# A graph-attention kernel on one core: two loads put behind the twelfth store of G, batch 1's row flags computed in the loop and sent through memory

## The chip, the cores and the metric

The kernel runs on one core of one Trainium2 chip, in float32. The metric is device time in microseconds (us) of one execution; the core's engines are TensorE (PE: matmuls, with PEld for its weight loads), VectorE (DVE), ScalarE (ACT), GpSimd (POOL) and SyncE (SP), which issues most of the DMAs.

## The reference

Sixteen batches of 512 rows with 512 features each. `v` is x, `q` one vector per batch, `adj` an integer tensor with 11 labels per pair; NONGT is 20, H is 16.

```python
row_zero = v.sum(-1) == 0
q_exp = where(row_zero[..., None], 0.0, q[:, None, :])
self_feat = concatenate([v, q_exp], -1) @ W_self.T + b_self
output = self_feat
for d in range(2):
    A = (adj_f if d == 0 else swapaxes(adj_f, 1, 2))[:, :, :NONGT, :]
    cond, vb = A.sum(-1), A @ w_bias + b_bias
    # attention of 512 queries over the first 20 rows, 16 heads of 32
    aff = einsum('bnhd,bmhd->bnhm', qh, kh) / sqrt(32)
    aff = where(cond > 0, aff, -9e15) + vb
    w = softmax(aff, -1)
    output += per-head projection of (w @ self_feat[:, :20]) by Wout[d] + bout[d]
return v + relu(output)
```

The row flags of this document are the negation of `row_zero`: the query vector enters a row of `self_feat` only where the row of x has a sum other than zero.

## The kernel before, in words

Features lie on the partitions, in four chunks of 128 (`C`); a batch's 512 rows are the columns, worked in four tiles of 128 (`nt` 0 to 3).

**Setup** (lines 458 to 777). The weights are loaded, the features of the 20 key rows of all batches are computed, and Wq is folded into the keys: `keys(runs)` (667) makes G, the keys of all batches as seen from the features, in 20 bursts `n` = 0 to 19 of TensorE products into two pairs of PSUM banks. ACT and DVE evict a burst into staging tiles `st` (four buffers), and SP stores each finished stage to memory, two stores to each of the 16 stages (698, 699). Between the bursts a list `plan` (721) sets other work for TensorE, by letters: m, b, c biases; v, w the projected values (`values`, 640); n the row flags (`row_flags`, 211); p the seven products of batch 0's `self_feat`. Lines 752 to 777 hang work of other engines on single bursts: masks (`mask_mul`, `mask_count`, `mask_sum`, `mask_spread`), `row_sums(1)`, `x_sum`, `clear_first` and `spill`.

**Row flags.** For batches 0 and 1, `row_sums` adds the four chunks of x on POOL; `row_flags` multiplies a 128x128 tile of ones with the sum, which leaves each row's total on all 128 partitions, and DVE compares with zero straight into `nz`. From batch 2 on ACT sums rows of x in another layout, POOL compares (`row_mask`, 195), SP stores the 512 flags to memory (198) and loads them back to all partitions (`load_nz`, 200).

**self_feat by seven products.** `product(b, n)` (250) computes a batch's features by a Strassen-like scheme of seven half-size products with sums of x blocks (`x_sum`, POOL). Products 1, 6, 7 and 4 accumulate in two banks `ps_a`; after each of them DVE reads the banks as they stand, with the flags: `partial` (285) adds `nz * qw` and writes a block of `sf`. Each further product onto `ps_a` waits for the partial before it. Product 2 goes to `ps_d`, 5 and 3 to `ps_c`; `joined` adds them.

**The main loop** (797). For each tile: the scores of 128 rows against G in two halves (`scores`, 349; 32-output products, four abreast), then `weigh` on DVE (add to the mask tile `full`, maximum, subtract), `expo` on ACT, and one tile later `normal` (sum and reciprocal on DVE, multiply on POOL) and `turn` (DVE transpose). At `nt` = 2 the previous batch is finished: `attend` (426) multiplies transposed weights with the projected values `vd`, in six runs of four products per batch, 32 or 64 outputs wide, and `finish` adds, applies relu and stores. The products of batch b+1 are woven in: 1 and 2 at `nt` = 2, with the first partial run by DVE between the maximum and the subtraction of that tile (939); 6, 7 and 5 at `nt` = 3; 4 and 3 at `nt` = 0 of the next batch.

**The order of everything is written by hand** (`manual_schedule`): each engine's instructions and SP's DMAs go out in program order. `behind` adds a wait that ties a load to an instruction of the loop. A DMA on SP also waits for the landing of the DMA eight places before it.

**Values' way.** The projected values `vw_d` are copied into a block pattern `bd_d` in memory, over zeros (`clear_first`, `clear_rest`), by small DMAs: `spill` (184) issues the next ones of a list. For the first five batches there are twelve: six from POOL in bursts 14 to 19 (765), six from POOL at `nt` = 0 of batch 0 (862).

**Memory pools.** After setup the pools `soft`, `gp`, `work`, `xsum` and `ident` (780 to 784) lie, in that order, over memory that setup used; a first write waits for the last use of what was there.

Of the kernel before, what the change touches and what calls it, by code (L numbers as in the profile page):

```python
# [7 lines left out]
F32 = mybir.dt.float32  # L8
I32 = mybir.dt.int32
AF = mybir.ActivationFunctionType  # L10
ALU = mybir.AluOpType
AX = mybir.AxisListType

P = 128
# [4 lines left out]
def gat_kernel(  # L19
# [20 lines left out]
    nc = tc.nc  # L40
    B, F, N = xT.shape
# [166 lines left out]
        for k in range(2, C):  # L208
            nc.gpsimd.tensor_add(t, t, xs[b][:, k])

    def row_flags(b):
        ps = bank(f"ps_nz{b}")
        nc.tensor.matmul(ps[:, :N], ones, rss[b], start=True, stop=True)  # L213
        nzs[b] = load.tile([P, N], F32, tag="nz", name=f"nz{b}")
        nc.vector.tensor_scalar(nzs[b], ps[:, :N], 0.0, None, ALU.not_equal)


    def weight_sums():
# [207 lines left out]
    def attend(b, banks, tiles=slice(0, NT), start=True, stop=True):  # L426


        wt = wts[b][:, tiles].rearrange("p t (g w) -> p (t g) w", g=HL)
        vd = vds[b].rearrange("p e i g -> p (e i g)")  # L430
        for first, runs in ((True, ((0, 1, 0), (3, 1, 2), (4, 1, 2), (7, 1, 4))), (False, ((1, 2, 1), (5, 2, 3)))):
            for at, n, j in runs:
                for a in range(HL):
                    r = bass.ts(a, R)
                    nc.tensor.matmul(  # L435
                        banks[a][bass.ds(at // 2 * DH, n * DH)].rearrange("p (t n) -> p t n", n=32),
                        vd[r, bass.ds(at * DH, n * DH)], wt[r, :, bass.ts(j, 32)],
                        start=start and first, stop=stop and not first,
                    )
# [18 lines left out]
    with tc.tile_pool(name="setup", bufs=1) as sp, tc.tile_pool(name="ps_acc", bufs=4, space=PSUM) as acc["pool"]:  # L458
# [18 lines left out]
        with tc.tile_pool(name="setup_k", bufs=1) as sk:  # L477
# [46 lines left out]
            nc.sync.dma_start(bo_sb, bout)  # L524
            for d in range(2):
                rows(wo_sb[:, d], woT[d])
            load_x(1)
            load_adj(0, 1)


            nc.gpsimd.tensor_add(rsk, xkv[:, 0], xkv[:, 1])
# [86 lines left out]
        with tc.tile_pool(name="setup_g", bufs=4) as sg:  # L618
# [82 lines left out]
            def block_product(n):  # L701
# [11 lines left out]
                "b": [(biases, ())],  # L713
                "c": [(bias_scores, (d,)) for d in range(2)],
                "m": [(bias_terms, (d, c)) for c in range(C) for d in range(2)],
                "n": [(row_flags, (b,)) for b in range(2)],
                "p": [(block_product, (n,)) for n in (1, 2, 6, 7, 5, 4, 3)],
                "v": [(values, (t, (d,), k)) for t in range(2) for d in range(2) for k in range(C)],
                "w": [(values, (2, (0, 1), k)) for k in range(C)],
            }  # L720
            plan = "mmvv bvv vvc vvc vvn vvw vvw vw wn p p p p p p p".split()

            units = [(fc, hg, d, b) for fc in range(C) for hg in range(C) for d in range(2) for b in range(B)]
            bursts = []
# [11 lines left out]
            for n, runs in enumerate(bursts):  # L736
                for i in range(len(rest)):
                    if i < (4 if n == 0 else 1) or any(fc == 0 and (d, hg) == rest[0] for fc, hg, d, _, _ in runs):
                        key_rows(*rest.pop(0))
                if n == 4:  # L740
                    values(*steps["v"].pop(0)[1])
                keys(runs)
                if rest:
                    for kind in "mm" if n else ():
                        f, args = steps[kind].pop(0)
                        f(*args)
                    continue
                first = n if first is None else first
                for kind in plan[n - first] if n - first < len(plan) else ():
                    f, args = steps[kind].pop(0)  # L750
                    f(*args)
                if n == 7:
                    mask_mul(0, 0)
                if n == 8:
                    mask_count(0, 0)
                if n == 10:
                    mask_sum(0, 0)
                    load_cq(0)
                if n == 7:
                    clear_first()  # L760
                if n == 9:
                    row_sums(1)
                    copies = blocks(0)
                if n > 13:
                    spill(1, nc.gpsimd)
                if n == 11:
                    new_self(0)
                    for i in range(1, 5):
                        x_sum(0, i)
                if 10 < n < 15:  # L770
                    mask_spread(0, 0, (n - 11,))
                if n == 14:
                    mask_mul(0, 1)
                if n == 15:
                    mask_count(0, 1)
                if n == 17:
                    full_add(0, 0)

    acc["pool"] = ctx.enter_context(tc.tile_pool(name="ps_loop", bufs=1, space=PSUM))
    soft = ctx.enter_context(tc.tile_pool(name="soft", bufs=2))  # L780
    gp = ctx.enter_context(tc.tile_pool(name="gp", bufs=2))
    work = ctx.enter_context(tc.tile_pool(name="work", bufs=2))
    xsum = ctx.enter_context(tc.tile_pool(name="xsum", bufs=1))
    ident = ctx.enter_context(tc.tile_pool(name="one", bufs=1)).tile([P, P], F32, name="ident")

    with tc.manual_schedule():
# [10 lines left out]
        for b in range(B):  # L797
# [7 lines left out]
            for nt in range(NT):  # L805
# [13 lines left out]
                if nt == 0:  # L819
# [39 lines left out]
                        turn(*prev)  # L859
                    full_add(b, 1)  # L860
                    if b == 0:
                        spill(6, nc.gpsimd)
                    if more:
                        x_sum(b + 1, 1)
                        load_adj(b + 1, 0, done["xsum"], slice(1, 2))
# [41 lines left out]
                if nt == 2:  # L907
# [22 lines left out]
                        load_xn(b + 2, 1, done["sum"], slice(1, 2))  # L930
                    if more:
                        load_keys(b + 1, range(1), done["normal"])
                    for g in range(2):
                        scores(b, nt, g, ps[g])
                    if more:
                        product(b + 1, 1)
                        product(b + 1, 2)
                        new_self(b + 1)
# [147 lines left out]
```

## Time and profile before

| what | value |
|---|---|
| device time, median of 3 runs | 583.28 us (582.72 to 583.82) |
| the profiled execution | 582.57 us |
| its span, first to last instruction | 580.7 us |
| mean granted TensorE clock | 0.999 |
| DMA, mean over the span | 212 GB/s, 123.26 MB |

A row of the chain of waits has the start in us from the span's start, the length, and the engine, tile and line. A row of a timeline has start, length, engine, line, operation and tiles, with the idle time ahead of it and what ended it in brackets. A row of the stretches has the stretch, its length, the busy time of each engine with the count of its instructions, the granted clock, and share and rate of the DMA.

### The profile page before, as it was taken

Reading aid. Unit: us, or ns where it says so; the run is one execution under the profiler, and the core shown is the slowest. Engines: PE = TensorE matmul, PEld = TensorE weight load, DVE = VectorE, ACT = ScalarE, POOL = GpSimd, SP = SyncE. Lnnn points to the kernel's source line nnn. Section 1 sums busy time; section 2 is a strip of 40 time slices with the busy share of each in tenths; the row PEclk is TensorE's granted clock in tenths of the full one; section 3 lists DMA queues with packets and bytes.
Section 4 is the critical chain, followed back from the end, with each engine's and each line's share of the span. In section 5 each row is a group of like instructions: output and inputs, shape, how many; then the busy total and the mean of one; then the engine's idle time right before and its main releaser. Section 6 shows DMA issues by size and latency. Waiting matters only on the chain.

```text
span 580.7 us, 30994 instructions
## 1 busy us (share of the span) xinstructions
PE 574.0 (99%) x13496; PEld 431.6 (74%) x13496; DVE 489.8 (84%) x786; ACT 395.8 (68%) x1170; POOL 404.2 (70%) x383
## 2 busy tenths in 40 slices
PE   8999999999999999999999999999999999999996
PEld 6444458878878787878778787887887878787873
DVE  0475676979898989898999999898989898989896
ACT  1334454587877777778786868687887877777671
POOL 2626976748687776858585867786868677685875
PEclk9999999999999999999999999999999999999999
DMA  8998997857675767777576767566657666674404
GB/s 290 387 399 300 332 362 274 231 144 222 202 239 177 215 200 198 218 181 229 171 215 166 219 166 219 166 205 181 202 162 223 197 191 182 196 205 109 148 19 146
DMA packets 98787, 123.26 MB, mean 212 GB/s; under 512 B 18876, under 2 KB 66968, under 8 KB 96604
## 3 DMA queue, kind: packets, MB, share of 16 engines
q1 hardware_dynamic: 96124, 117.80, 65.5%
q0 software_dynamic: 1392, 2.43, 1.8%
q8 instruction: 106, 1.74, 1.2%
q10 hardware_dynamic: 1136, 1.06, 0.5%
q14 instruction: 29, 0.24, 0.1%
HBM read 82.30 MB, written 40.24 MB: 211 GB/s over the span
## 4 chain that ended last, share of the span: by engine, by line
PE 94%; DVE 3%; DMA 1%; issue 0%; POOL 0%; SPq 0%; ACT 0%; DVEq 0%; POOLq 0%; ACTq 0%
PE ps_s L365 45%; PE ps_a L283 19%; PE ps_c L283 9%; PE ps_o L435 5%; PE ps_d L283 5%; PE ps_v L649 3%; PE ps_k L588 3%; DMA ws_q<-in_wsT 1%; PE ps_kv L537 1%; DVE o L444 0%; PE ps_nz L213 0%; DVE o L1023 0%; DVE wt L424 0%; DVE ps_s L383 0%; DVE sm L415 0%
## 5 line engine op out<-in xcount | busy, mean ns | idle before, releaser
L365 PEld LDWEIGHTS ps_s<-g,sf 128*32 128x32 f32 x8192 | 263.0, 110 | 21.5 <-issue 13.9
L365 PE MATMUL ps_s<-g,sf 128*32 128x152 f32 x8192 | 278.1, 293 | 0.3 <-issue 0.2
L337 ACT COPY both<-add 32x80 f32<-32x80 f32 x512 | 130.9, 256 | 60.3 <-DVE add L328 54.4
L417 POOL TENSOR_TENSOR s<-s,sm 128x640 f32<-128x640 f32 x63 | 80.2, 1274 | 95.5 <-DVE sm L416 73.4
L344 POOL TENSOR_TENSOR full<-cq,both 128x640 f32<-128x640 f32 x64 | 100.3, 1567 | 27.1 <-issue 21.2
L317 ACT ACTIVATE prod<-adj,wb_sb 128x80 f32<-128x80 int32 x330 | 112.4, 432 | 0.0
L392 ACT ACTIVATE s<-s 128x640 f32<-128x640 f32 x63 | 46.5, 738 | 56.5 <-DVE s L387 56.1
L449 POOL TENSOR_TENSOR o<-o,x 128x512 f32<-128x512 f32 x60 | 76.6, 1299 | 0.0
L379 DVE TENSOR_TENSOR full<-ps_s,full 128x608 f32<-128x608 f32 x63 | 48.7, 773 | 22.5 <-PE ps_s L365 19.2
L283 PE MATMUL ps_a<-t,ws_s 128*32 128x246 f32 x1024 | 60.0, 371 | 0.0
L415 DVE TENSOR_REDUCE sm<-s 128x32 f32<-128x640 f32 x63 | 50.8, 807 | 10.6 <-ACT s L392 10.4
L383 DVE TENSOR_REDUCE ps_s<-full 128x32 f32<-128x640 f32 x63 | 52.2, 828 | 2.2
L424 DVE STREAM_TRANSPOSE wt<-s 128x640 f32<-128x640 f32 x63 | 52.8, 838 | 0.6 <-POOL s L417 0.6
L387 DVE TENSOR_TENSOR s<-full,ps_s 128x640 f32<-128x640 f32 x63 | 51.5, 818 | 1.1
L289 DVE SCALAR_TENSOR_TENSOR sf<-nz,qw,ps_a 128x246 f32<-128x246 f32 x128 | 51.6, 443 | 0.3
L283 PEld LDWEIGHTS ps_a<-t,ws_s 128*32 128x32 f32 x1024 | 33.9, 110 | 17.5 <-issue 0.9
L328 DVE TENSOR_REDUCE add<-prod 128x80 f32<-128x960 f32 x32 | 36.8, 1149 | 6.8 <-ACT prod L317 4.0
L446 ACT ACTIVATE o<-o,bo 128x512 f32<-128x512 f32 x60 | 38.2, 709 | 0.6 <-DVE o L444 0.6
L248 POOL TENSOR_TENSOR t<-x 128x492 f32<-128x492 f32 x32 | 36.7, 1148 | 1.6 <-DMA g_d<-st 1.5
L248 POOL TENSOR_TENSOR t<-x,t 128x492 f32<-128x492 f32 x32 | 36.7, 1148 | 1.3
L435 PE MATMUL ps_o<-wt,vd 32*32 32x512 f32 (+5 forms) x816 | 37.6, 578 | 0.0
L444 DVE TENSOR_TENSOR o<-ps_o,sf 128x512 f32<-128x512 f32 x60 | 36.7, 668 | 0.0
(225 smaller groups left out, 712.6 us busy)
## 6 DMA issues: line engine op xcount, KB each, us to landing
g<-g_d SPq DMA_DIRECT2D x60, 304.0 KB
g_d<-st SPq DMA_DIRECT2D x16, 1064.0 KB
out_T<-o SPq DMA_DIRECT2D x60, 256.0 KB
xn<-in_xn SPq DMA_DIRECT2D x56, 256.0 KB
x<-in_xT SPq DMA_DIRECT2D x56, 256.0 KB
adj<-in_adj SPq DMA_DIRECT2D x60, 220.0 KB
nz<-nz_d SPq DMA_DIRECT2D x14, 256.0 KB
wk<-in_wkT SPq DMA_DIRECT2D x2, 1024.0 KB
```

Of the source, the lines that this page charges most:

```text
L248: done["xsum"] = nc.gpsimd.tensor_sub(t, one, two)
L283: nc.tensor.matmul(to, lhs, x[:, k], start=start, stop=stop, skip_group_check=n != 2)
L289: done["partial"] = nc.vector.scalar_tensor_tensor(to[:, i], nzs[b][:, half(l)], qw[:, 2 * f + i, b : b + 1], parts[b, "a"][i][:, :HN], AL ...
L317: nc.scalar.activation(p[:, :, l], a[:, :, l], AF.Identity, scale=wb_sb[:, l : l + 1])
L337: done["spread"] = nc.scalar.copy(adds[b, h][bass.ts(a, R), :, g], add[r].rearrange("p (t m) -> p t m", t=2))
L344: done["full"] = nc.gpsimd.tensor_add(f, cqs[b].unsqueeze(1).to_broadcast(shape), adds[b, nt // 2][:, nt % 2].unsqueeze(2).to_broadcast(sh ...
L365: nc.tensor.matmul(to, sfs[b][:, k, bass.ds(nt * P + (2 * g + j) * R, R)], of, start=(onto is None and k == 0 and (whole or j == 0)), stop ...
L383: nc.vector.tensor_reduce(mx, f, AX.X, ALU.max)
L417: done["normal"] = nc.gpsimd.tensor_mul(s, s, sm.unsqueeze(3).to_broadcast(full))
L424: nc.vector.transpose(wts[b][:, nt], s.rearrange("p a h m -> p (a h m)"))
L435: nc.tensor.matmul(banks[a][bass.ds(at // 2 * DH, n * DH)].rearrange("p (t n) -> p t n", n=32), vd[r, bass.ds(at * DH, n * DH)], wt[r, :, ...
L449: nc.gpsimd.tensor_add(o[:, c], o[:, c], xs[b][:, c])
```

## The change

Five edits:

- The loads of batch 1's x and of the second half of batch 0's masks (`load_x(1)`, `load_adj(0, 1)`) move from the head of SP's queue to burst 15, behind the twelfth store of G; `clear_first` moves there from burst 7. What follows from them moves too: `mask_mul(0, 1)` from burst 14 to 18, `mask_count(0, 1)` and `row_sums(1)` to burst 19.
- The row flags are made by four products of 32 outputs by 128 columns. DVE compares a 128x128 tile, SP stores one row of each 32 (`nz_d`), and `load_nz` brings them back to all partitions. Batch 0's load stands at burst 10. Batch 1's flags move into the loop, to `nt` = 2 of batch 0: product ahead of the scores, load behind them.
- All twelve spills of the first five batches go out from SP at `nt` = 0 of batch 0.
- `attend` starts with the 64-output products and ends with the 32-output ones.
- The pool `xsum` is placed ahead of `work`. One step of `values` comes a burst earlier.

```diff
-    def row_flags(b):
-        ps = bank(f"ps_nz{b}")
-        nc.tensor.matmul(ps[:, :N], ones, rss[b], start=True, stop=True)
-        nzs[b] = load.tile([P, N], F32, tag="nz", name=f"nz{b}")
-        nc.vector.tensor_scalar(nzs[b], ps[:, :N], 0.0, None, ALU.not_equal)
+    def row_flags(b, at=None):
+
+        ps = bank(f"ps_nz{b}", at)
+        for a in range(HL):
+            nc.tensor.matmul(ps[bass.ts(a, R), :P], ones[:, :R], rss[b][:, bass.ts(a, P)], start=True, stop=True)
+        t = msk.tile([P, P], F32, tag="nzf", name=f"nzf{b}", bufs=1)
+        nc.vector.tensor_scalar(t, ps[:, :P], 0.0, None, ALU.not_equal)
+        nc.sync.dma_start(nz_d[b].rearrange("(a n) -> a n", a=HL), t[0:P:R])
...
-        for first, runs in ((True, ((0, 1, 0), (3, 1, 2), (4, 1, 2), (7, 1, 4))), (False, ((1, 2, 1), (5, 2, 3)))):
+        for first, runs in ((True, ((1, 2, 1), (5, 2, 3))), (False, ((0, 1, 0), (3, 1, 2), (4, 1, 2), (7, 1, 4)))):
...
-            load_x(1)
-            load_adj(0, 1)
...
-                "n": [(row_flags, (b,)) for b in range(2)],
+                "n": [(row_flags, (0,))],
...
-            plan = "mmvv bvv vvc vvc vvn vvw vvw vw wn p p p p p p p".split()
+            plan = "mmvv bvv vvc vvc vvn vvw vw vw w p p p p p p p".split()
...
-                if n == 4:
+                if n in (3, 4):
                     values(*steps["v"].pop(0)[1])
...
                     load_cq(0)
-                if n == 7:
+                    load_nz(0)
+                if n == 15:
+                    load_adj(0, 1)
+                    load_x(1)
                     clear_first()
-                if n == 9:
-                    row_sums(1)
                     copies = blocks(0)
-                if n > 13:
-                    spill(1, nc.gpsimd)
...
-                if n == 14:
-                    mask_mul(0, 1)
-                if n == 15:
-                    mask_count(0, 1)
                 if n == 17:
                     full_add(0, 0)
+                if n == 18:
+                    mask_mul(0, 1)
+                if n == 19:
+                    mask_count(0, 1)
+                    row_sums(1)
...
+    xsum = ctx.enter_context(tc.tile_pool(name="xsum", bufs=1))
     work = ctx.enter_context(tc.tile_pool(name="work", bufs=2))
-    xsum = ctx.enter_context(tc.tile_pool(name="xsum", bufs=1))
...
                     if b == 0:
-                        spill(6, nc.gpsimd)
+                        spill(12)
...
                         load_keys(b + 1, range(1), done["normal"])
+                    if b == 0:
+                        row_flags(1, 3)
                     for g in range(2):
                         scores(b, nt, g, ps[g])
+                    if b == 0:
+                        load_nz(1)
                     if more:
                         product(b + 1, 1)
                         product(b + 1, 2)
```

## The prediction

> **What bounds the kernel now.** I read the page first, then the chain of waits in order of time, then the timelines of SP, POOL, DVE and ACT from 88 to 130 us, where the change acts.
>
> ```profile
> span 580.7 us, 30994 instructions
> PE 574.0 (99%) x13496; PEld 431.6 (74%) x13496; DVE 489.8 (84%) x786; ACT 395.8 (68%) x1170; POOL 404.2 (70%) x383
> PE 94%; DVE 3%; DMA 1%; issue 0%; POOL 0%; SPq 0%; ACT 0%; DVEq 0%; POOLq 0%; ACTq 0%
> ```
>
> 94% of the chain that ended last is matmul time. TensorE works from end to end, so a microsecond for which it waits is a microsecond of the kernel, and work elsewhere counts only if it makes TensorE wait. The chain, in order of time (start, length, what):
>
> ```profile
> 56.51 1.06 PE ps_nz L213 x2
> ...
> 70.07 1.06 PE ps_nz L213 x2
> ...
> 91.33 3.85 PE ps_s L365 x114
> ...
> 106.32 1.66 PE ps_d L283 x32
> 107.98 1.62 PE ps_a L283 x30
> 109.60 4.05 PE ps_s L365 x124
> ...
> 129.17 2.68 PE ps_o L435 x41
> ...
> 160.28 2.17 PE ps_o L435 x48
> ...
> 170.04 1.66 PE ps_a L283 x32
> ...
> 190.75 2.17 PE ps_o L435 x48
> ```
>
> The reader is to see three things. The two row-flag products of setup stand on the chain with 1.06 us each. The main loop begins at 91.33. And the pieces of batch 1 follow one another without a hole: product 2 (ps_d) at 106.32, product 6 (ps_a) at 107.98. From product 6 to the next attend the first pass takes 129.17 - 107.98 = 21.19 us and a later batch 190.75 - 170.04 = 20.71; from attend to attend it is 31.11 against 190.75 - 160.28 = 30.47. So 0.48 + 0.64 = 1.1 us of small waits is all that could ever be caught up after product 6.
>
> **The change, part by part.**
>
> *Flags in TensorE.* 2 x 1.06 = 2.12 us of 128-output products go. In their place stand, per batch, four products of 32 outputs by 128 columns, which lie side by side in the array as the score products do (the L365 piece at 109.60: 124 instructions of 152 columns, four abreast, in 4.05 us, so 0.13 us for four; a product is two instructions): an estimate of 0.25 us, so 0.5 for both. One moves into the loop. The filler behind one burst of key products shrinks to four value products; if its evictions then show, I charge them with 0.3. The loop then begins 1.5 us earlier, at 89.8. Moving eight value products to burst 3 changes no sum.
>
> *The flags' way.* Before, the product gave the flags to all 128 partitions and DVE wrote them straight to nz. Now DVE makes a 128x128 tile, SP stores four of its rows to memory, and SP loads them back, spread over the partitions. For batch 0 this happens in setup, with bursts to spare. For batch 1 the store and the load stand in the same step (nt = 2 of batch 0) as their consumer: the first partial of batch 1, which DVE runs between maximum and subtraction, and behind which product 6 waits because it adds to the bank that the partial reads. This is the step that decides. DVE first:
>
> ```profile
> 91.99 1.14 DVE L328 TENSOR_REDUCE add<-prod 128x80 f32<-128x960 f32 x1
> ...
> 105.97 0.83 DVE L383 TENSOR_REDUCE ps_s<-full 128x32 f32<-128x640 f32 x1
> 106.71 0.84 DVE L289 SCALAR_TENSOR_TENSOR sf<-nz,qw,ps_a 128x246 f32<-128x246 f32 x2
> ```
>
> The partial ran at 106.71; with the earlier start DVE would be there at about 105.7. When are the flags there? The queue of SP decides, and it is in order:
>
> ```profile
> 95.32 5.42 SPq L119 DMA_DIRECT2D adj<-in_adj  x2
> 100.83 0.38 SPq L157 DMA_DIRECT2D bd_d<-zero  x1
> 101.30 1.94 SPq L124 DMA_DIRECT2D cq<-cq_d  x4
> 103.34 1.99 SPq L119 DMA_DIRECT2D adj<-in_adj  x2
> 105.39 0.38 SPq L157 DMA_DIRECT2D bd_d<-zero  x1
> 106.19 1.55 SPq L113 DMA_DIRECT2D xn<-in_xn  x3
> 107.85 0.38 SPq L135 DMA_DIRECT2D g<-g_d  x1
> ```
>
> In the changed program the store of the flags stands right behind that last load of keys, which waits for POOL's normalisation of the second tile. POOL's side of it, with ACT's spread of the masks, which releases the first of these loads:
>
> ```profile
> 93.16 2.13 ACT L337 COPY both<-add 32x80 f32<-32x80 f32 x8 [2.54 <-DVE add L328]
> ```
> ```profile
> 93.70 4.10 POOL L187 DMA_DIRECT2D bd_d<-vw_d  x6
> 99.33 1.05 POOL L248 TENSOR_TENSOR t<-x 128x492 f32<-128x492 f32 x1 [1.53 <-DMA g_d<-st]
> ...
> 106.12 1.27 POOL L417 TENSOR_TENSOR s<-s,sm 128x640 f32<-128x640 f32 x1
> ```
> ```profile
> L209 POOL TENSOR_TENSOR rx<-rx,x 128x512 f32<-128x512 f32 x4 | 5.1, 1276 | 0.3
> L187 SPq DMA_DIRECT2D bd_d<-vw_d x12: 775/802/1084, 187.4 to 257.9; - x12
> ```
>
> Step by step. The mask count of batch 0 now runs in the last burst, between the last joined and the mask sum, with one reduction on DVE and one small operation on POOL (an estimate of 1.7 us: the reduction like the one of L328, 1.14, over eleven of its twelve columns, and 0.6 for the other): the sum ends at about 93.5 instead of 93.13, the spread at 95.7, and the first mask load goes out there. Behind it now stand twelve spills that POOL used to issue. On SP a spill of 44 blocks (four chunks by eleven batches) took 0.80 us and a plain load 0.38; these have 20 blocks, so I take 0.5 each: 6 us. The second mask load goes out at about 102.5 instead of 100.41. Twelve more transfers follow up to and with the keys, at 0.45 each (the four of cq took 1.94): 108.0. POOL loses 4.10 us of spills and gains 3 x 1.28 = 3.8 of input sums, and the wait for G's stores of 1.53 goes because the sums lie elsewhere; its normalisation ends at about 105.8 instead of 107.39, so POOL is not the later of the two. The store of the flags goes out at **108.4**; bounds 106.3 (POOL alone) and 112 (spills at 0.80).
>
> How long is a store followed by a load that waits for it? The loop of before has the same pair for batches from 2 on, and in three of them SP stood waiting for the store:
>
> ```profile
> SPq L202 <- DMA nz_d<-nz: 1.6, 3, 1.0
> ```
> ```profile
> 397.05 0.38 SPq L198 DMA_DIRECT2D nz_d<-nz  x1
> ...
> 401.43 0.33 SPq L202 DMA_DIRECT2D nz<-nz_d  x1
> ```
> ```profile
> 4.23 0.33 SPq L499 DMA_DIRECT2D xkv<-in_xkvT  x1
> ```
> ```profile
> SPq L499 <- DMA ws_v<-in_wsT: 1.7, 1, 1.7
> ```
> ```profile
> 0.72 0.91 ACTq L499 DMA_DIRECT2D ws_v<-in_wsT  x2
> ```
>
> The store took 401.43 - 397.05 = 4.4 us. The load moves 256 KB; a weight load of that size, issued at 0.72 on idle queues, released SP at 4.23, so 3.5 us; I take 4, since inputs and keys were issued just ahead. Nothing shorter is shown, so 3.5 + 3.5 is my lower end for the pair, and 4.8 + 5 the upper. The flags land at 108.4 + 4.4 + 4.0 = 116.8; half a partial (0.42) and a wake-up later product 6 starts at **117.4**, where it started at 107.98: **+9.4 us**. TensorE ends product 2 at about 106.3 and has nothing else in its order, so it stands for 11 us. The 1.5 us won in setup are inside this hole and buy nothing.
>
> The Trainium skill (DMA: Bandwidth & Descriptors, Anatomy of one DMA) gives a fixed cost of about 2.0 us per DMA plus bytes over 436 GB/s. By it the pair would be 2.0 + 2.6 us and product 6 would start near 113.5, +5.5; the 4.4 us measured for a store of 2 KB speaks against it.
>
> *The clock after the hole.*
>
> ```profile
> 575.05 0.96 PE L435 MATMUL ps_o<-wt,vd 32*32 32x128 f32 x48
> ```
> ```profile
> 576.00:579.00 3.00, 0.01 (x1) 0.00 (x0) 0.91 (x5) 0.00 (x0) 0.00 (x0) 1.00 0.99 334
> 579.00:580.70 1.70, 0.00 (x0) 0.00 (x0) 0.00 (x0) 0.00 (x0) 0.00 (x0) 0.52 0.10 28
> ```
> ```profile
> 1.05 3.35 PE L496 MATMUL ps_warm<-ones 128*128 128x128 f32 x14 [1.05 <-DVE ones L482]
> ```
> ```profile
> 573.96 1.16 PE L789 MATMUL ps_o<-biased,ident 128*128 128x128 f32 x8
> ```
>
> The granted clock (the third column from the end) is 1.00 in the three microseconds behind the last matmul and 0.52 after them: three idle microseconds are enough to lose half of it. At the start fourteen 128x128 instructions take 3.35 us, 0.24 each, where eight take 1.16 at the end, 0.15: the array was slow for at least that long. A hole of 11 us so costs a second start at half speed, at least 3.35 / 2 = 1.7 us; I take **+2**, and nothing is the lower end, if the hole stays short. The Trainium skill (TensorE: Matmul & The Clock Gate, What's actually happening) has the array at half clock after an idle window of about 3.4 us and until one busy window of the same length; by it the price is 1.7.
>
> *Loads behind the twelfth store.* Batch 1's x, half of batch 0's masks and the zeros now enter a busy queue at about 77 us. I expect the masks at about 85 and x at 88; ACT casts the masks at about 86 and POOL sums x at 92. Cost zero; if they come 3 us later, the last evictions wait by as much, before the hole, which absorbs most of it.
>
> *Wide output first.* The same 48 instructions and the same three changes of tile shape per attend, in another order. Streaming alone, at the rate of the scores (0.86 ns a column), 4 x 512 columns would be 1.76 of the 2.17 us; the other 0.41 are the three changes. I take zero; if one change goes or one is added, it is 0.14 x 15 = 2.1 us either way.
>
> **Sum.** +9.4 + 2 - 1.1 (all small waits caught up) = +10.3 us on the profiled execution of 582.57 (580.7 of span and 1.9 around it). That run lies 0.7 below the median of 583.28; the difference should be the same, so 593.6.
>
> **The rivals.**
>
> 1. *The round trip is short.* The store goes out at 106.3 and the pair takes 5 to 7 us: product 6 at 112 to 114, the clock loss small. +3 to +6, 586 to 589. For it: POOL is then free. Against: twelve spills on SP and the 4.4 us store.
> 2. *The hole doesn't open: faster.* If the flags were there when DVE reaches the partial (105.7), the 1.6 us of TensorE time (2.12 - 0.5) would count and the time would be 583.28 - 1.6 = 581.7. The deciding point: a store issued by about 98, ahead of the keys. The order of SP speaks against it, since the mask load of 95.7 and twelve spills are ahead.
> 3. *The spills choke SP.* At 0.80 us each and with waits for G's stores, the store of the flags goes out at 112 or later into a queue full of inputs: product 6 at 121 to 124, +15 to +18.
> 4. *The change doesn't do what it says*, the narrow flags costing as much as the wide: hidden in the hole, no change to the forecast.
>
> **Chances.** Forecast 0.65, rival 1 0.15, rival 3 0.10, rival 2 0.06, a time within 0.2% 0.04 (0.2%, or 1.2 us, is about what a measurement of this kernel tells from no change). Faster 0.06, same 0.04, slower 0.90. The range takes the ends: from rival 1's lower part, 586, to +16, 600.
>
> **What would show it.** In the profile after: a hole of about 11 us in TensorE's chain ahead of the second use of ps_a by batch 1, at 106 to 117 us, with DVE's L289 partial waiting for the DMA of nz; a granted clock of half just behind it; SP's twelve spills in a row at about 96 to 102 us; from then on the chain of before, shifted. The main loop begins near 89.8. The prediction is wrong if the partial of batch 1 starts by 108, or if the steady batches change their 30.47 us.

## The result and the profile after

The changed kernel takes **600.26 us** (599.37 to 601.4, 5 runs) against 582.96 (582.41 to 583.82, 5 runs) for the kernel before beside it: ratio 1.0298 [1.0281, 1.0315], or 17.3 us slower. The prediction was 593.6, with a range to 600.0: the sign and the mechanism came true, and the loss is 7 us larger than forecast. The profiled execution took 600.26 us. One of the twelve executions of experiment 7 took 907.92 us, at a granted clock of 0.61, and is left out of that experiment's figures.

First the page of the changed kernel: span, busy time, and the chain's shares by engine.

```profile
span 598.3 us, 31025 instructions
PE 575.0 (96%) x13508; PEld 433.6 (72%) x13508; DVE 489.0 (82%) x786; ACT 395.9 (66%) x1170; POOL 395.5 (66%) x371
PE 89%; issue 3%; DMA 3%; POOL 2%; DVE 1%; SPq 1%; ACT 0%; DVEq 0%; POOLq 0%
```

The span is 17.6 us longer, while TensorE's busy time is 1.0 us longer: the loss is standing time. The chain of the changed kernel, in order of time (start, length, what), shows where:

```profile
110.85 1.50 POOL full L347
112.35 12.12 issue
124.47 3.51 PE ps_a L286 x32
127.97 4.84 PE ps_s L368 x128
132.82 1.67 PE ps_a L286 x32
```

There is one long hole, ahead of batch 1's product 6, which starts at 124.47 instead of 107.98 (+16.5). The chain passes through GpSimd up to 112.35 and so shows 12.12 us of the hole; TensorE itself had ended product 2 at 110.6 and stood 13.86 us, as its timeline shows (in brackets the idle time ahead of the row):

```profile
124.47 3.51 PE L286 MATMUL ps_a<-t,ws_s 128*32 128x246 f32 x32 [13.86 <-issue]
```

Behind the hole the chain is that of before. The attends of the changed kernel, from the chain:

```profile
147.74 2.47 PE ps_o L438 x48
...
178.63 2.17 PE ps_o L438 x48
...
209.10 2.17 PE ps_o L438 x48
```

From attend to attend it is 209.10 - 178.63 = 30.47 us, to the hundredth the 30.47 of before, and an attend of a steady batch takes the same 2.17. The first of these attends starts 18.57 us later than before, the second and the third 18.35: behind the second attend the change adds nothing.

What ends the hole stands in DVE's timeline of the changed kernel (in brackets the idle time ahead of a row and what ended it), and why it ends so late in SP's:

```profile
101.54 0.82 DVE L390 TENSOR_TENSOR s<-full,ps_s 128x640 f32<-128x640 f32 x1 [3.93 <-PE ps_nz L215]
...
108.67 0.23 DVE L217 TENSOR_SCALAR nzf<-ps_nz 128x128 f32<-128x128 f32 x1
...
123.89 0.85 DVE L292 SCALAR_TENSOR_TENSOR sf<-nz,qw,ps_a 128x246 f32<-128x246 f32 x2 [13.45 <-DMA nz<-nz_d]
```
```profile
96.28 0.33 SPq L119 DMA_DIRECT2D adj<-in_adj  x1
96.70 13.09 SPq L187 DMA_DIRECT2D bd_d<-vw_d  x12
109.90 0.46 SPq L119 DMA_DIRECT2D adj<-in_adj  x1
...
115.45 0.38 SPq L135 DMA_DIRECT2D g<-g_d  x1
115.92 0.58 SPq L218 DMA_DIRECT2D nz_d<-nzf  x1
120.82 0.32 SPq L202 DMA_DIRECT2D nz<-nz_d  x1
```

DVE stood 13.45 us for the flags of batch 1. DVE had made them by 108.9 (the row of the flag tile starts at 108.67 and takes 0.23), but the store stood on SP behind twelve spills of 13.09 us and the loads behind those, and went out at 115.92; the load waited 4.9 us more for the store, and the flags landed 3.07 us after that. Each of these twelve spills on its own (shortest, median, longest, in ns):

```profile
L187 SPq DMA_DIRECT2D bd_d<-vw_d x12: 706/723/2878, 96.7 to 109.1; - x12
```

The median is 0.72 us; the third and the fifth took 2.45 and 2.88. The clock behind the hole, from the view by stretches (the third column from the end):

```profile
112.35:124.47 12.12, 0.00 (x1) 0.03 (x1) 0.57 (x2) 3.81 (x12) 0.00 (x0) 0.64 0.58 178
124.47:129.28 4.81, 4.81 (x58) 3.15 (x62) 4.78 (x9) 0.74 (x1) 1.93 (x3) 0.50 0.37 106
```

Product 6 ran at half clock, 3.51 us, where it takes 1.87 behind a wait at full clock (experiment 4), and the clock was back after 4.81 us of work. The Trainium skill (TensorE: Matmul & The Clock Gate, What's actually happening) would have the array back after at least one busy window of about 3.4 us, and the 4.8 measured here agree with that.

### The profile page after: what moved, and what is told of

It reads as the page before. It is cut to its first block, busy times and chain, and to the rows that moved or that the text cites. A ratio compares the mean times of both kernels' runs of the same rounds, so it can differ in the third digit from the quotient of the medians.

```text
span 598.3 us, 31025 instructions
## 1 busy us (share of the span) xinstructions
PE 575.0 (96%) x13508; PEld 433.6 (72%) x13508; DVE 489.0 (82%) x786; ACT 395.9 (66%) x1170; POOL 395.5 (66%) x371
## 3 DMA queue, kind: packets, MB, share of 16 engines
q10 hardware_dynamic: 1136, 1.06, 0.5%
## 4 chain that ended last, share of the span: by engine, by line
PE 89%; issue 3%; DMA 3%; POOL 2%; DVE 1%; SPq 1%; ACT 0%; DVEq 0%; POOLq 0%
PE ps_s L368 44%; PE ps_a L286 18%; PE ps_c L286 9%; PE ps_o L438 6%; PE ps_d L286 4%; PE ps_k L589 3%; DMA ws_q<-in_wsT 1%; PE ps_v L650 1%; DMA cq_d<-c 1%; PE ps_kv L538 1%; PE ps_o L790 1%; POOL cq_d L636 0%; DMA cq<-cq_d 0%; POOL prod L317 0%; SPq L124 0%
## 5 line engine op out<-in xcount | busy, mean ns | idle before, releaser
L418 DVE TENSOR_REDUCE sm<-s 128x32 f32<-128x640 f32 x63 | 50.8, 807 | 10.2 <-ACT s L395 9.9
```

## The experiments

Differences are given against the kernel before, measured beside each group (583.05 in the first, 583.29 in the second, 583.0 and 583.31 in the last two). The first four undo one part of the change each, or fill the hole.

**1. Batch 1's flags without the trip.** One wide product in the loop, read straight into nz; the rest as changed.

```diff
-                        row_flags(1, 3)
+                        wide_flags(1, 3)     # the product and comparison of before, in bank 3
...
-                    if b == 0:
-                        load_nz(1)
```

> The changed kernel, but batch 1's flags come from one 128-output product in the loop that DVE compares straight into nz: no store, no load. Theory 1 (the hole is the flags' way behind the spills on SP): the 13.4 us for which DVE waits for the DMA of nz are gone. What is late next is the second half of batch 1's masks, which leave SP behind the twelve spills at about 110 us: ACT's mask products end at about 116, its third exponential at 117, and product 7 of batch 1 starts at about 119.5 where it started at 113.8 before the change. Time 586 to 589, no slow clock. Rival (the flags are only one of several equal causes, and the masks behind the spills hold the array nearly as long): 594 to 598. Rival 2 (the flags were all): 582 to 584.

Measured 590.09 (588.92 to 590.36), ratio 1.0115 [1.01, 1.013]: 10.2 us of the loss are gone, a little less than the theory asked. TensorE's timeline of this run, products 6 and 7:

```profile
112.78 1.87 PE L293 MATMUL ps_a<-t,ws_s 128*32 128x246 f32 x32 [1.24 <-POOL s L427]
119.61 1.87 PE L293 MATMUL ps_a<-t,ws_s 128*32 128x246 f32 x32 [0.82 <-DVE sf L299]
```

TensorE waits 1.24 us ahead of product 6 instead of 13.86, and the product runs at full clock. The store and load of the flags were the hole. Product 7 starts at 119.61, where the theory put it. But product 6 is still 4.8 us later than before, so there is a second cause ahead of it. DVE's timeline of this run has a candidate:

```profile
103.00 0.82 DVE L397 TENSOR_TENSOR s<-full,ps_s 128x640 f32<-128x640 f32 x1 [5.87 <-PE ps_nz L224]
```

The first soft tile waits 5.87 us for the flags' product, as it waited 3.93 in the changed kernel (experiment 5 asks why). That this wait makes the whole 4.8 us was not tried by itself.

**2. Spills and value zeros issued by GpSimd, as before**, the rest as changed.

```diff
+                if n == 7:
+                    clear_first()
+                if n == 9:
+                    copies = blocks(0)
+                if n > 13:
+                    spill(1, nc.gpsimd)
...
-                        spill(12)
+                        spill(6, nc.gpsimd)
```

> The changed kernel, but the zeros and the twelve spills are issued by POOL as before the change: the zeros in burst 7, six spills in bursts 14 to 19, six at the first tile; the flags still go through memory. Theory 1 (13.1 us of spills on SP ahead of the store): the keys' load now waits for POOL's second normalisation at about 111 to 112, not for SP; the flags' store goes out at 111.5 to 112.5 instead of 115.9, product 6 starts at 119.5 to 120.5 instead of 124.5, and the time falls by 4 to 5, to 595 to 597. Rival (the spills only shift a queue that is anyway full, store and load take what is left): no change, 599 to 601. Rival 2 (the spills are the whole loss): 585 to 588.

Measured 596.61 (596.45 to 597.44), ratio 1.0234 [1.0219, 1.0249], as the theory said. SP's timeline:

```profile
112.43 0.53 SPq L218 DMA_DIRECT2D nz_d<-nzf  x1
118.07 0.33 SPq L202 DMA_DIRECT2D nz<-nz_d  x1
```

The store goes out 3.5 us earlier and the time is 3.7 us shorter. It isn't the whole 13 us of the spills, because SP's loads of masks then wait for GpSimd's sums (8.2 us in this run), which stand behind the spills there.

**3. Batch 1's input and half the masks at the head of SP's queue, as before**, the rest as changed.

```diff
+            load_x(1)
+            load_adj(0, 1)
...
-                    load_adj(0, 1)
-                    load_x(1)
                     clear_first()
```

> The changed kernel, but batch 1's x and half of batch 0's masks are loaded at the head of SP's queue as before the change; all else as changed. Theory 1: the waits of ACT for the masks and the stage buffer (0.9 and 1.8 us) are gone, the loop begins at about 90 instead of 92, the spills find G's stores landed and take 9 to 10 us instead of 13.1; the store of the flags goes out at 111 to 112 and the time falls by 3.5 to 5.5, to 595 to 597. Rival (where the loads stand costs nothing, since the hole absorbs it): 599.5 to 601.

Measured 596.96 (596.41 to 597.55), ratio 1.0237 [1.0222, 1.0252], as the theory said: 3.3 us. The main loop begins at 89.84 here and at 90.80 in the changed kernel, which has a wait of 0.60 and then one of 0.27 there for the last evictions. SP's timeline of this run:

```profile
96.19 10.13 SPq L187 DMA_DIRECT2D bd_d<-vw_d  x12
...
112.44 0.58 SPq L218 DMA_DIRECT2D nz_d<-nzf  x1
```

The same twelve spills take 10.13 us instead of 13.09. A DMA on SP waits for the one eight places before it. Counted back from the two long spills of the changed kernel, these are stores of G that went out at 84.94 and 86.97, behind the moved loads. That the moved loads made these stores land late is argued; it was not tried by itself.

**4. The hole filled.** The changed kernel with twelve extra 128x512 products behind product 2, whose result is not used; nothing is left out.

```diff
+                        if b == 0:
+                            fill = bank("ps_fill", 3)
+                            for _ in range(12):
+                                nc.tensor.matmul(fill, kvn[:, 0, :P], sfs[0][:, 0], start=True, stop=True)
```

> The changed kernel with twelve extra products of 128 by 512 (about 1.06 us each, 12.7 in all, results not used) on TensorE between products 2 and 6 of batch 1, that is inside its hole. Theory (the granted clock of one half behind the hole costs 2.4 us): the clock stays at 1.00, product 6 takes 1.7 instead of 3.5 us, the time falls by 2 to 2.6 to about 598. Rival (behind the hole DVE's chain sets the pace and the slow array costs nothing): 600 within 0.5. Rival 2 (the hole is shorter than the extra work): over 601.

Measured 599.93 (599.64 to 601.49), ratio 1.0295 [1.0276, 1.0314]: no gain, so the theory of 2 to 2.6 us falls and the rival holds. Its chain, and the clock of one stretch:

```profile
103.48 5.73 PE ps_s L368 x128
...
123.03 2.18 issue
125.21 1.87 PE ps_a L286 x32
...
147.11 2.70 PE ps_o L438 x46
```
```profile
103.00:106.40 3.40, 2.92 (x48) 2.30 (x52) 2.53 (x5) 2.77 (x9) 1.52 (x2) 0.50 0.34 68
```

Product 6 runs in 1.87 us, so the fill does keep the clock up; from product 6 to the attend it is 147.11 - 125.21 = 21.90 us against 23.27 in the changed kernel and 21.19 before. Of this gain of 1.4 us half is gone with product 6's start, 0.74 us later, and the 0.6 that are left at the attend are below what the measurement tells. So the slow clock costs about 1.4 us that a fill can win back, and this run does not show them in the total, because its spills began 0.43 us later and took 13.50 us for 13.09. The clock had already been low once in this run, at 103.0 to 106.4, behind waits of 1.73 and 0.91 us.

The second group asks for what is left, and turns to the kernel before.

**5. The ones in memory of their own**, so that the first soft tile does not wait 3.93 us for the flags' product; the rest as changed.

```diff
+    ones = const.tile([P, P], F32, name="ones")
...
-        ones = sp.tile([P, P], F32, name="ones")
```

> The changed kernel with one edit: the tile of ones that the flags' product reads lies in memory of its own, so the main loop's first soft tile and the first input sum no longer wait for that product (in the changed kernel VectorE waited 3.93 us for it at 101.5, GpSimd 3.09). Theory: these waits stand on the path only where GpSimd's normalisation of the second tile would have released the store of the flags, and it ended at 110.85 while SP came to the store at 115.92 after its loads; TensorE reaches the hole earlier and stands longer. So 599.5 to 600.5, no change, product 6 still at 123.5 to 124.5, the two waits gone, the hole longer by 1 to 2 us. Rival: the late soft tile delays all that follows in the first batch, and 596 to 597.5 comes out.

Measured 600.9 (599.77 to 601.99), ratio 1.0308 [1.0285, 1.033]: no gain. Its chain:

```profile
108.76 16.98 issue
125.74 3.51 PE ps_a L287 x32
```

Both waits are gone. TensorE reaches the hole 1.9 us earlier (108.76 for 110.6) and stands 3.1 us longer (16.98 for 13.86), as from store to partial the flags took 9.4 us here. The wait for the ones, new with the change and unforeseen, was covered by the hole; where the hole is gone, as in experiment 1, it is not covered.

**6. The kernel before with its twelve spills on SP at once**, none on GpSimd.

```diff
-                if n > 13:
-                    spill(1, nc.gpsimd)
...
-                        spill(6, nc.gpsimd)
+                        spill(12)
```

> The kernel before with one part of the change alone: all twelve spills issued by SP behind the first tile's softmax, none by GpSimd; flags, loads and filler as before. Theory (the spills cost 0.7 to 1.1 us each on SP whatever stands beside them, and what is queued behind them comes late by their sum): twelve in a row of 9 to 13 us, batch 1's masks land about 10 us later, the mask weighting of batch 1 on ScalarE waits for them as it waited 5.2 us in the changed kernel, and 587 to 590 comes out with no hole at the flags. Rival (SP has room there, and only the flags' way made its queue matter): within 0.7 of 583.0. In favour of something between: GpSimd gets 4 us back.

Measured 585.82 (585.07 to 587.13), ratio 1.005 [1.0031, 1.0068], between the two. SP's timeline and the waits of this run:

```profile
96.07 9.40 SPq L187 DMA_DIRECT2D bd_d<-vw_d  x12
```
```profile
ACT prod L317 <- DMA adj<-in_adj: 5.4, 1, 5.4
```

The spills cost 0.78 us each here, the mechanism is the expected one (batch 1's masks late, ScalarE waiting 5.4 us for them), and the price is 2.5 us; that it is no more fits with the 4.1 us that GpSimd gets back.

**7. The kernel before with narrow flags through memory for both batches, all in setup.** This is the prediction's second rival with its condition fulfilled: the flags are there in time.

```diff
     def row_flags(b, at=None):        # as in the changed kernel
...
                     load_cq(0)
+                    load_nz(0)
+                if n == 14:
+                    load_nz(1)
```

> The kernel before with the 32-output flags sent through memory for both batches, but all of it in setup: the products stand where the wide ones stood, each store behind its product, and the loads two and six bursts later, 15 us and more ahead of their readers. Theory (the narrow flags save TensorE time, 2 x 1.06 against about 0.5 us, and it was the place of the second round trip that cost): 1.0 to 1.8 us faster, 581.2 to 582.0, no hole. Rival (the saved products were hidden, or two more transfers on SP in setup eat it): 582.7 to 583.4.

Measured 584.9 (584.06 to 586.37), ratio 1.0035 [1.0023, 1.0047]: slower, and both expectations missed. Its chain, with the first flags' product in front, then the stretch from 93 to 100 us in this run and in the kernel before (third column from the end the clock, then the DMA engines' busy share):

```profile
56.67 0.22 PE ps_nz L215 x8
...
90.15 3.35 PE ps_s L368 x102
93.50 2.12 issue
...
99.96 1.13 issue
...
109.61 0.12 PE ps_a L286 x2
```
```profile
93.00:100.00 7.00, 4.84 (x141) 4.22 (x134) 2.44 (x3) 1.46 (x6) 3.62 (x6) 1.00 0.97 347
```
```profile
93.00:100.00 7.00, 6.72 (x200) 6.08 (x193) 2.86 (x5) 3.08 (x11) 5.47 (x8) 1.00 0.73 239
```

There is no hole at the flags. The narrow product takes 0.22 us for 1.06, close to the 0.25 of the prediction, and the loop does begin 1.2 us earlier (90.15 for 91.33); but TensorE then stands for 2.12 us in the middle of the first scores and for 1.13 behind them, and product 6 starts at 109.61, 1.6 us later than before. The DMA engines are busy for 0.97 of that stretch, 0.73 before. What exactly TensorE waited for, the profile doesn't show. Other versions have such a wait in the first scores too, again without a releaser: 0.24 us in the kernel before, 1.10 in the changed kernel, 2.20 in experiment 1. The share of the DMA engines alone doesn't set its length: in experiment 10 it is 0.98 in the same stretch, and the waits are 0.88 and 0.31.

**8. The changed kernel with its order on SP mended**: the loads first, the ones apart, the flags of batch 1 one tile earlier and their load at the head of `nt` = 2, the spills still on SP, in three groups of four behind that load.

```diff
-                    if b == 0:
-                        spill(12)
...
                     for g in range(2):
                         scores(b, nt, g, ps[g])      # nt = 1
+                    if b == 0:
+                        row_flags(1, 3)
...
                     else:
+                        load_nz(1)                    # nt = 2, b = 0
                         load_xn(2, 0, done["full"], slice(1, 2))
...
+                        if b == 0:
+                            spill(4)                  # at three places behind it
```

> The changed kernel with the causes found so far undone together, its parts otherwise kept (narrow flags through memory, sums in other memory, wide output first, filler moved): batch 1's input and half the masks loaded at the head of SP's queue as before, the ones in memory of their own, the flags of batch 1 computed behind the scores of the second tile and loaded back at the head of the third step, and the twelve spills, still on SP, in three groups of four behind that load. Theory (place in SP's queue is the whole cause, no price is left in the parts): the store goes out at 98 to 100, the load at 103 to 104.5, the flags land by 108, product 6 starts at 107 to 109 as before, and 582 to 585 comes out, 15 to 18 us less than the changed kernel. Rival (spills on SP or the flags' way cost several us wherever they stand): 588 or more.

Measured 589.29 (587.14 to 590.76), ratio 1.0106 [1.008, 1.0132]. 11 us are won, not the 15 to 18 that the theory asked, and the time is in the rival's range. SP's and DVE's timelines:

```profile
100.26 0.53 SPq L219 DMA_DIRECT2D nz_d<-nzf  x1
...
105.82 0.41 SPq L203 DMA_DIRECT2D nz<-nz_d  x1
```
```profile
111.02 0.85 DVE L293 SCALAR_TENSOR_TENSOR sf<-nz,qw,ps_a 128x246 f32<-128x246 f32 x2 [4.86 <-DMA nz<-nz_d]
```

The store goes out at 100.26, nearly as asked; the load goes out 5.6 us later, and takes 5.2. These 5.6 us are place in the queue again: eight other DMAs stand between the two, and SP's waits of this run have none for the store. The load's 5.2 us fall into a stretch in which the DMA engines are busy for 0.94 of the time. DVE waits 4.9 us for it. So place in the queue is most of the loss, but the trip keeps a price of its own even here.

The last two groups price the rest of the change.

**9. The kernel before with narrow flags and no trip**: four 32-output products over all 512 columns, side by side, for each batch.

```diff
-        nc.tensor.matmul(ps[:, :N], ones, rss[b], start=True, stop=True)
+        for a in range(HL):
+            nc.tensor.matmul(ps[bass.ts(a, R), :N], ones[:, :R], rss[b], start=True, stop=True)
```

> The kernel before with the flags' products alone made narrow, and no trip through memory: each wide product is replaced by four of 32 outputs over all 512 columns, side by side in the array, so that the flags still come to all 128 partitions and VectorE writes them straight to nz. Estimate from the score products (512 columns at 0.86 ns are 0.44 us against 1.06): 2 x 0.6 = 1.2 us of TensorE time in setup. Theory A (the DMA engines, busy for 0.93 to 1.04 of the time from 58 to 93 us in the kernel before, set when the first batch can go on; what TensorE saves in setup is stood off in the first tiles): no change, 582.8 to 583.5. Theory B (the saving counts, and in the run with both flags sent through memory in setup the two round trips' own 512 KB cost it): 581.8 to 582.3.

Measured 582.28 (581.42 to 583.16), ratio 0.9983 [0.9973, 0.9994]: 0.7 us faster than before, the upper end of theory B. It is the only version that beats both kernels. From the chain of this run, and from the waits of GpSimd:

```profile
56.62 0.86 PE ps_nz L214 x8
...
98.66 1.13 issue
```
```profile
POOL t L249 <- DMA g_d<-st: 3.3, 1, 3.3
```

Four narrow products of 512 columns take 0.86 us for 1.06, so setup saves 0.4 us for both batches and not the 1.2 of the estimate. The main loop begins 0.28 us earlier (91.05), but TensorE stands 1.13 us in the first scores, GpSimd waits 3.3 us for G's stores (1.53 before), and the second attend starts at 160.61, 0.33 us later than before. The profiled execution gets ahead only in later batches, of which two took 0.3 and 0.5 us longer than the others in the kernel before. So the time is lower, but that the narrow products made it so is not shown.

**10. The kernel before with two loads of 256 KB more in setup.**

```diff
+                if n in (10, 14):
+                    spare = load.tile([P, N], F32, tag="spare", name=f"spare{n}", bufs=1)
+                    nc.sync.dma_start(spare, xT[0, 0:1].partition_broadcast(P))
```

> The kernel before with two loads more in setup, 256 KB each, spread over the partitions like the load of the flags, into a tile that nobody reads, at the two places where the run with both flags in setup loads them; wide products as before. It leaves nothing out. Theory (the two transfers take 1.4 to 1.7 us from DMA engines that have no room there, at some 300 to 370 GB/s, and SP's share of setup ends later): 584.3 to 585. Rival (the queue has room, or what is late is not waited for): 582.8 to 583.6.

Measured 584.06 (583.37 to 585.08), ratio 1.0018 [1.0007, 1.0028]: 1.1 us, a little under the theory. The stretch from 93 to 100 us of this run has the DMA engines as full as experiment 7 had them:

```profile
93.00:100.00 7.00, 6.12 (x188) 5.80 (x182) 3.13 (x4) 2.05 (x8) 6.21 (x8) 1.00 0.98 352
```

Two transfers that nobody reads cost more than the 0.7 us of experiment 9. With -0.7 and +1.1 from these two runs experiment 7 should stand at most 0.4 us above before, since its products are shorter still; it stands 1.6 above. The 1.2 us or more between are open (its two stores and the later waits of SP in setup are candidates that were not tried).

**11. The kernel before with the two-wide outputs of `attend` first.**

```diff
-        for first, runs in ((True, ((0, 1, 0), (3, 1, 2), (4, 1, 2), (7, 1, 4))), (False, ((1, 2, 1), (5, 2, 3)))):
+        for first, runs in ((True, ((1, 2, 1), (5, 2, 3))), (False, ((0, 1, 0), (3, 1, 2), (4, 1, 2), (7, 1, 4)))):
```

> The kernel before with the attend's order alone changed: the two-wide outputs ahead of the one-wide ones. Theory (the same 48 instructions and the same number of changes of shape): no change, 582.8 to 583.5. Rival: one change of shape fewer or more in each of 15 attends, 0.14 us each, 2.1 us to one side.

Measured 583.6 (582.72 to 584.28), ratio 1.0007 [0.9997, 1.0016]: no change, as expected. An attend of a steady batch in this run's chain takes the 2.17 us of before:

```profile
161.28 2.17 PE ps_o L435 x48
```

**12. The changed kernel with four causes undone at once**: the trip of batch 1's flags (by the products of experiment 9), the place of the two loads, the spills on SP, the shared memory of the ones.

```diff
-                        row_flags(1, 3)
+                        side_flags(1, 3)
...
-                        load_nz(1)
...
+            load_x(1)
+            load_adj(0, 1)
...
-                        spill(12)
+                        spill(6, nc.gpsimd)       # and six in setup
```

> The changed kernel with all the causes found so far undone at once: batch 1's flags by four narrow products over all 512 columns, read by VectorE straight into nz, so without store and load; batch 1's input and half the masks at the head of SP's queue; the spills and the value zeros issued by GpSimd as before; the ones in memory of their own. What stays of the change: batch 0's narrow flags through memory, batch 1's flags in the loop, the mask product of batch 0 in the last bursts, the input sums in other memory, the filler moved, wide output first. Theory (these four hold the whole loss): no wait for nz, product 6 at 107 to 109, 582.3 to 584.5. Rival (something else of the change costs too, the late mask product or the place of the input sums): 586 or more, with a wait in the first two tiles that the kernel before doesn't have.

Measured 585.25 (583.81 to 586.8), ratio 1.0028 [1.0013, 1.0042]: 15 of the 17.3 us are undone; 0.75 us above what the theory allowed. Product 6 starts at 109.84, 1.9 us later than before. Two waits of the chain ahead of it, and what the weight load of product 6 waited for:

```profile
94.57 1.31 issue
...
109.29 0.55 issue
```
```profile
PEld ps_a L295 <- POOL t L260: 1.0, 1, 1.0
```

The first is the wait in the first scores again, 1.31 us for 0.24 before, with no releaser. At the second GpSimd is the later one: the sums of batch 1's x, which the change puts into the last burst, and the six spills fall together at 93 to 103 us, and its input sums come 1.0 us late. That the late row sums so carry a small price of their own is argued from these rows; it was not tried by itself.

## Why the prediction was right and wrong

*Right:* the mechanism, with its place. The hole stands ahead of product 6, TensorE stands 13.86 us for the 11 forecast, DVE's partial waits for the load of nz, the store waits on SP behind the spills and the loads after them, the clock is at half behind the hole, and the steady batches keep their 30.47 us. Taking the trip away gave back 10.2 us (experiment 1).

*Wrong:* the size. Term by term, on the profiled executions:

| step | forecast | measured |
|---|---|---|
| main loop begins | 89.8 | 90.80 |
| mask spread ends, first mask load goes out | 95.7 | 96.25, load at 96.28 |
| twelve spills on SP | 6.0 | 13.09 |
| from second mask load to store of the flags | 5.9 (102.5 to 108.4) | 6.0 |
| store goes out | 108.4 | 115.92 |
| store until its load goes out | 4.4 | 4.9 |
| load until the partial | 4.0 | 3.07 |
| product 6 starts | 117.4 (+9.4) | 124.47 (+16.5) |
| clock | +2 | +2.55, product 6 to 7: 8.35 us for 5.80 |
| small waits caught up | -1.1 | -0.7 by the second attend, -1.4 by the end |
| sum | +10.3 | +17.6 of span |

Of the 1.4 us caught up, the 0.7 behind the second attend are no work of the change: in the profiled execution of the kernel before, two batches took 30.75 and 30.93 us from attend to attend (from 282.18 and from 434.83) where the others take 30.47.

**The step that failed is "these have 20 blocks, so I take 0.5 each: 6 us".** The prediction quoted the row of 0.80 us for a spill on SP and scaled it down by its blocks. The runs show that it hardly scales: 0.72 us in the median for 20 blocks in the changed kernel, where 44 blocks take 0.80; twelve in a row take 9.40 us in experiment 6, and four 3.03 to 3.20 in experiment 8. So 3.4 of the 7.1 us too little are the size of a spill. The other 3.7 are waits of two spills for earlier transfers, by the count of experiment 3 stores of G; the term put them at nothing, and the twelve go down to 10.13 us when the two loads are moved back. Both halves stood in the text, as rival 3 (0.80 us each, waits for G's stores, product 6 at 121 to 124) with a chance of 0.10; measured were 13.09 us and 124.47. The 7.1 us of this one term are the difference between forecast and result; errors of 0.6 us in the spread and of 0.4 in the pair nearly cancel.

**"Loads behind the twelfth store: cost zero"** was wrong too. The masks landed at 88.9 where 85 was expected, as ScalarE's row in the changed kernel shows:

```profile
88.88 0.94 ACT L316 CAST prod<-adj 128x880 f32<-128x880 int32 x1 [1.76 <-DMA adj<-in_adj]
```
Experiment 3 prices the move at 3.3 us; they are paid in the spills' waits and in the start of the loop, and so inside the terms above.

**"Its normalisation ends at about 105.8, so POOL is not the later of the two"** held only by luck of size. GpSimd's normalisation ended at 110.85, because the first input sum and DVE's first soft tile waited for the flags' product, which reads the ones in memory that they take over. The prediction didn't see this wait at all. It costs nothing in the changed kernel, as experiment 5 shows, since SP came later still; with the hole gone it is a candidate for what is left (experiment 1).

**"+2 for the clock"** is right locally (2.55 up to product 7); up to the next attend the fill of experiment 4 wins 1.4 us back, which its total doesn't show. **"Wide output first: zero"** held (experiment 11). The time of a store with its load was put well, 8.0 us for 8.4 forecast; the estimate by the Trainium skill (DMA: Bandwidth & Descriptors, Anatomy of one DMA), a section on DMAs that GpSimd issues, was 4.6 for the pair. In the five runs in which SP waited for the store (the changed kernel and experiments 2 to 5) the trip took 7.8 to 9.4 us, and none comes near 4.6.

**Rival 2's price (581.7, faster by 1.6) was wrong even where its condition holds.** With the flags in time the kernel is at 584.9 (experiment 7). TensorE does save 1.7 us there (0.22 for 1.06, twice), and 1.2 of them are still there when the loop begins, but waits in the first scores, whose cause is open, take more than that. Two loads that nobody reads cost 1.1 us by themselves (experiment 10). The prediction had counted setup as TensorE's alone; the DMA engines are as full there, for 0.93 to 1.04 of the time from 58 to 93 us in the kernel before.

The loss, by what undoing it gave back in separate runs: the trip 10.2, the spills on SP 3.7, the two loads 3.3, the ones 0. These do not simply add up, since what one wait covers another one shows; all four undone at once give back 15 of the 17.3 (experiment 12).

## What to carry to other kernels

A transfer in an in-order queue costs what stands ahead of it, so price each DMA that is moved into a queue by the row of its like there, without scaling it down by bytes or blocks unless two rows show that it scales; then look for the first consumer behind the last of them. A result that goes to memory and back needs the whole trip, here 7.8 to 9.4 us, between its maker and its reader, and no more than a product of 1 us was to be saved by it. When an engine is said to be the bound, look also at the share of the DMA engines in the same stretch: of the 1.2 us by which the loop began earlier in experiment 7, nothing was left at product 6.

## What the runs showed of the hardware

- A DMA from memory to memory in many short rows holds SP for 0.71 to 0.88 us where nothing is waited for, almost whatever its size (0.72 us for one of 10 KB, 0.73 for one of 50 KB in experiment 6, both of 20 blocks; 0.80 in the median for 44 blocks in the kernel before); a plain load holds it for 0.32 to 0.46.
- The load of 256 KB that spreads one row of 2 KB over all partitions took 3.07 us in the changed kernel, where the DMA engines were busy for 0.25 of just these 3.07 us, and 5.2 in experiment 8, where they were busy for 0.94 of its 5.2 us.
- TensorE's clock fell to 0.50 in a hole of 13.86 us. In experiment 4 it also fell to 0.50, behind two waits of 1.73 and 0.91 us with 1.2 us of work between them; in experiment 1, behind waits of 2.20 and 0.91 us with 2.0 us of work between them, it stayed at 1.00, as this row shows. What separates the two cases is open.

```profile
103.88:108.00 4.12, 4.12 (x128) 4.12 (x132) 3.27 (x5) 2.75 (x9) 2.24 (x3) 1.00 0.22 35
```
